# Two transformer branches on one core: first tiles without the keys that do not exist, a bound on rows of short TensorE instructions, and a new set of planner numbers

## The chip, the core and the metric

One core of a Trainium2 chip runs the whole program: one launch, inputs in HBM, output in HBM. The core has five engines with queues of their own: TensorE (PE in the profile; PEld is its weight loading), VectorE (DVE), ScalarE (ACT), GpSimd (POOL) and SyncE (SP), which issues nearly all transfers. The metric is device time in microseconds (us).

## What is computed

`x` is (4, 1024, 256), f32. It is normalised, goes through two independent branches, and the three are added.

```python
x = L0_attn_x
xn = _layernorm(x, axis=-1)
x = x + _L0_attn_ref(xn, ...) + _L0_ffn_ref(xn, ...)

# first branch: rms norm, 16 heads of 64, window 64
scores = einsum('bhnqd,bhnkd->bhnqk', qb, kctx) * scale   # 64 queries, 2 x 64 keys
diff = Bk + qi - kj
base = (diff >= 0) & (diff <= window)
key_exists = (blk - 1) * Bk + kj[None] >= 0
attn = softmax(where(base & key_exists, scores, NEG))
out = einsum('bhnqk,bhnkd->bhnqd', attn, vctx) * sigmoid(gates)
return out.reshape(b, S, HEADS * DIM_HEAD) @ W_out

# second branch: 2 layers, 8 heads of 64, window 128
h = shift_token(x)                       # half the features one token later
q, k, v = split(h @ wqkv)                # q, k: l2 norm, scale, rotation
mask = (i < j) | (i > j + WINDOW) | (j == -1)
attn = softmax(where(mask, -max, q @ k.T));  x = x + (attn @ v) @ wo
h = layernorm(shift_token(x)) * lg + lb
a, g = split(h @ w1 + b1);  x = x + (a * gelu(g)) @ w2 + b2
```

A block of queries sees its own block of keys and the one before. For the first block of a sequence the one before does not exist, and the mask (`key_exists`, `j == -1`) excludes it.

## The kernel before

**Tiling.** The 4 sequences of 1024 tokens are cut into 16 blocks of 256 tokens (`TB`), 4 a sequence (`g` counts them), and each block into 2 tiles of 128 tokens (`i`). `first_attention(n)` does the first branch of block `n`; `layer(l, n)` does the attention of layer `l` of the second branch for block `n`, and `after_attention` its second half. The loops at the end of `layers_kernel` call the first branch for all blocks, then layer 0, then layer 1, with the last three blocks of the first branch mixed with the first of layer 0.

**The planner.** These functions issue nothing. Each calls `op(us, fn, r, w, a, ...)`, which records an operation (`fn` emits its instructions), its estimated time on each engine that can do it, and what it reads and writes. When all are recorded, `Plan.run` simulates the engines with these estimates and fixes one order for each engine and the buffer of each tile; then `Plan.emit` calls the functions in that order. At each step it takes, for each engine, the waiting operation with the smallest `score`: its due time, plus `IDLE` times the time that the engine would stand idle until the operation can begin, plus `TURN` if it needs another mode than the one before (on PE `full` for matmuls on the whole 128x128 array, `rc` for those on 64x64 quarters). `RATE` and `LAND` give a transfer's planned time, `LAT` the delay from an operation's end to its users, `SLACK` a factor on an engine's times, `LOOK` how far ahead in the recorded order an operation may be taken, and the last table of `Plan(...)` how many buffers of a kind are kept for older operations.

**Attention on TensorE.** All matmuls are f32. One matmul of the program shows as two matmul records in the profile, each with a weight load. In the first branch a tile of 128 tokens is done for 4 pairs of heads at a time (`q4`, two groups): `sa` (`scores`, L798) makes the scores, 16 matmuls on 64x64 quarters; DVE adds the mask and takes the minimum (L824); ACT does the exponential (L834); POOL weighs (L853); a transfer out and back and a DVE transpose (`across`, `turn_in`, L464, L473, L481) turn the result; `oa` (`attend`, L887) multiplies by the values, 24 matmuls in three pieces: (1) 128 queries by the keys of the tile, (0) the first 64 queries by the 64 keys before them, (2) the last 64 queries by the last 64 keys. In the second branch a tile has 8 heads: `sb` (L1118), 16 matmuls with 192 key columns (`WB`), the same chain (L1139, L1153, L1173, `across`), and `ob` (L1208), 32 matmuls in four pieces. The first tile of a sequence (`opens`, or `g == 0 and i == 0`) runs the same instructions as any other: keys and values of the missing block are zeros, and a second mask excludes them. L1463 (`last`) is the other place with 64x64 matmuls, 4 for a block.

**Everything else on TensorE** is `full`: projections to queries and keys (L764, `qka`), values and gates (L675, `va`), out (L922, `pr`); in the second branch L979 (`qkvb`), L1233 (`pw`), L1403 (`up`) and L1449 (`down`).

**The start.** `load_x(0)` brings the first block. DVE and POOL make its statistics, DVE normalises it (L643). For blocks 0 and 1 (`EARLY`) `across` is called with `near`: PE transposes the four pieces into a PSUM bank (L427), ACT or DVE copies the bank to the tile `hT` (L452), and `scaled` multiplies `hT` in place by gamma (L658 on ACT). Then the projections begin (L764, L675).

Of the kernel before, what the change touches and what calls it, by code (L numbers as in the profile page):

```python
# [44 lines left out]
N_D = 12  # L45
RATE = 540.0
LAND = 3.7
LAG = 2
# [22 lines left out]
class Op:  # L71
    __slots__ = (
        "us", "fn", "bufs", "mode", "out", "rank", "lat", "left", "ready", "users", "done",
        "start", "end", "eng", "name", "n", "due",
    )


class Plan:
    LAT = {"PE": 0.25, "DVE": 0.30000000000000004, "ACT": 0.30000000000000004, "POOL": 0.30000000000000004, "SP": 2.0}
    SLACK = {"DVE": 1.05, "POOL": 1.05, "ACT": 1.15}  # L80
    SWITCH = {"PE": 0.1, "ACT": 1.4}
    TURN = {"PE": 3.0, "ACT": 40.0}
    IDLE = 300.0
    LOOK = 120.0
    DEAR = {"DVE": 3.0}
# [9 lines left out]

    def op(self, us, fn, r=(), w=(), a=(), mode=None, out=None, lat=None, name=""):


        o = Op()
        o.us, o.fn, o.mode, o.lat, o.name = us, fn, mode, lat, name  # L100
        o.out = out or mode
        o.rank, o.n = self.rank, len(self.ops)
        if "PE" in us:
            self.rank += us["PE"]
        o.users, o.done, o.ready = [], False, 0.0
        deps = set()
        for b in r:
            deps.update(b.writers)
            b.readers.append(o)
        for b in w:  # L110
            deps.update(b.writers, b.readers)
            b.writers, b.readers, b.base = [o], [], [o]
        for b in a:
            deps.update(b.readers, b.base)
            b.writers = b.writers + [o]
        deps.discard(o)
        o.bufs = list({id(b): b for b in (*r, *w, *a)}.values())
        for b in o.bufs:
            b.left += 1
        for d in deps:  # L120
            d.users.append(o)
        o.left = len(deps)
        self.ops.append(o)
        return o

    def run(self):
# [13 lines left out]
        for o in self.ops:  # L140
            if not o.left:
                enter(o)
        oldest, out = 0, []

# [16 lines left out]
        while len(out) < len(self.ops):  # L161
# [4 lines left out]
            for e in engines:  # L166
                picks = []
                for o in waiting[e]:
# [13 lines left out]
                    if turn and e in self.SWITCH:  # L182
                        t += self.SWITCH[e]
                    score = o.due + self.IDLE * (t - at[e]) + (self.TURN[e] if turn else 0.0)
                    picks.append((score, o.n, t, o))
                if picks:
# [9 lines left out]
            for other in o.us:  # L196
                waiting[other].remove(o)
            o.done, o.start, o.end, o.eng = True, t, t + o.us[e] * self.SLACK.get(e, 1.0), e
            at[e] = o.end
# [28 lines left out]
def layers_kernel(  # L228
# [41 lines left out]
        },  # L270
        {"w": (4, 0.1, 30), "g": (1, 0.0, 1), "s": (4, 0.05, 12), "ps": (0, 0.02, 3), "d": (1, 0.0, 1)},
    )
# [31 lines left out]

    load_x(0)

    early = fixed([P, 2], "early")
# [298 lines left out]
    def first_attention(n, before):  # L606
# [44 lines left out]
        hT = buf("w")  # L651
        across(hn, 4, [(hT, lambda b: b.t[:, :512].rearrange("p (k c j) -> p j k c", k=4, j=4), 0, 4)], n in EARLY)

        def scaled(e):
            for c in range(NC):
                at = slice(c * TB, (c + 1) * TB)
                if e == "ACT":
                    nc.scalar.mul(hT.t[:, at], hT.t[:, at], gam.t[:, c : c + 1])  # L658
                else:
                    nc.vector.tensor_scalar_mul(hT.t[:, at], hT.t[:, at], gam.t[:, c : c + 1])  # L660

        op({"ACT": 0.9, "DVE": 0.95}, scaled, r=(gam,), w=(hT,), name="hT")
        H = lambda c, i: hT.t[:, c * TB + i * P : c * TB + (i + 1) * P]
# [87 lines left out]
        for q4 in range(PA // GA):  # L751
# [37 lines left out]
            for i in range(NT):  # L789
# [15 lines left out]

                op({"PE": 0.88}, scores, r=(*qd, *kd, *(() if i else (fk[q4],))), w=pss, mode="rc", name="sa")
                sTs, sm = [], buf("s")
# [69 lines left out]

                def attend(e, po=po, sTs=sTs, vs=vts[i], q4=q4):

                    for n, (k, at, m, to) in enumerate(  # L880
                        ((1, WA, P, 0), (0, 0, WA, 0), (2, 3 * WA, WA, WA))
                    ):
                        for h in range(2):
                            for z in range(2):
                                for j in range(2):
# [4 lines left out]
                                        sTs[j].t[r, h * TB + at : h * TB + at + m],  # L890
                                        start=(h == 0 and n == 0), stop=(h == 1 and n == 2),
                                    )

                op(
                    {"PE": 0.94}, attend,
                    r=(*sTs, *{id(v[q4]): v[q4] for z in vts[i] for v in z}.values()), w=po,
                    mode="rc", name="oa",
                )
# [37 lines left out]
    def layer(l, n, before):  # L936
# [33 lines left out]
        for i in range(NT):  # L970
# [139 lines left out]

            def scores(e, pss=pss, qT=qT, kx=kx):
                for hf in range(2):
                    for u in range(2):
                        for blk in range(2):
                            at = (2 * hf + u) * P + blk * D
                            for j in range(2):
                                r = slice(j * D, (j + 1) * D)
                                nc.tensor.matmul(  # L1118
                                    v2(pss[hf][j], 2, WB)[blk * D : (blk + 1) * D, u],
                                    qT.t[r, at : at + D],  # L1120
                                    v2(kx[hf], 2, 2 * P)[r, u, blk * D : blk * D + WB],
                                    start=True, stop=True,
                                )

            op(
                {"PE": 1.3}, scores, r=(qT, *kx), w=(*pss[0], *pss[1]), mode="rc", name="sb",
            )
            mk = mask_b.t[:, int(opens), :]
            sTs = [[], []]
            for hf in range(2):  # L1130
                sm, exs = buf("s"), []
                for j in range(2):
                    s, ex = buf("w"), buf("w")
                    exs.append(ex)

                    def least(e, s=s, sm=sm, ps=pss[hf][j], hf=hf, j=j, rn=rn, mk=mk):
                        for u in range(2):
                            h = 4 * hf + 2 * u + j
                            nc.vector.tensor_tensor_reduce(  # L1139
                                v2(s, 2, WB)[:, u], v2(ps, 2, WB)[:, u],  # L1140
                                mk, rn.t[:, h : h + 1], BIG,
                                ALU.add, ALU.min, sm.t[:, 2 * j + u : 2 * j + u + 1],
                            )

                    op(
                        {"DVE": 0.69}, least, r=(pss[hf][j], mask_b, rn), w=(s,), a=(sm,),
                        name="min",
                    )


                    def expo(e, s=s, ex=ex, sm=sm, j=j):
                        for u in range(2):
                            nc.scalar.activation(  # L1153
                                v2(ex, 2, WB)[:, u].rearrange("p (a k r) -> p k a r", k=3, a=2),
                                v2(s, 2, WB)[:, u].rearrange("p (k a r) -> p k a r", k=3, a=2),
                                AF.Exp, bias=sm.t[:, 2 * j + u : 2 * j + u + 1], scale=-1.0,
# [11 lines left out]
                for j, ex in enumerate(exs):  # L1168

                    def weigh(e, ex=ex, sm=sm, j=j):  # L1170
                        for u in range(2):
                            at = 8 + 2 * j + u
                            nc.gpsimd.tensor_scalar(  # L1173
                                v2(ex, 2, WB)[:, u], v2(ex, 2, WB)[:, u],
                                sm.t[:, at : at + 1], 1.0, ALU.mult, ALU.mult,
# [6 lines left out]
                    across(  # L1182
                        ex, 3,
                        [(
                            sT,
                            lambda b: bass.AP(
                                tensor=b.t.tensor, offset=b.t.offset,
                                ap=[[*b.t.ap[0]], [16, 4], [P, 3], [WB, 2], [1, 16]],
                            ),
                            0, 3,  # L1190
                        )],
# [4 lines left out]

            def attend(e, po=po, sTs=sTs, v=((vt_old, vs, vt, vs_next), (vs_old, vt_old, vs, vt))):


                for n, (k, at, m, to) in enumerate(  # L1200
                    ((1, P, P, 0), (2, 2 * P, P, 0), (0, 0, D, 0), (3, 3 * P + D, D, D))
                ):
                    for hf in range(2):
                        for u in range(2):
                            for j in range(2):
# [7 lines left out]
                                    sTs[hf][j].t[r, at : at + m],  # L1213
                                    start=(hf == 0 and n == 0), stop=(hf == 1 and n == 3),
                                )

            op(
                {"PE": 1.45}, attend, r=(*sTs[0], *sTs[1], vt, vt_old, vs, vs_old, vs_next), w=po,
                mode="rc", name="ob",
            )  # L1220
# [32 lines left out]
    def after_attention(l, n, w, y2, y2_old, ts):  # L1253
# [213 lines left out]

        op({"PE": 0.45}, down_last, r=(gT[-1], w["w2"][-1]), a=(*pzs.values(),), mode="rc", name="last")
        for i, pz in pzs.items():
# [136 lines left out]
```

## Time and profile before

| | |
|---|---|
| time, median of 3 runs | 1722.07 us (1716.95 to 1726.0) |
| time of the profiled execution | 1720.48 us |
| its span, first to last instruction | 1718.7 us |
| mean granted TensorE clock | 1.000 |
| records of the L798 and L887 groups | 2048 and 3072 |
| records of the L1118 and L1208 groups | 2048 and 4096 |
| PE idle from 0 to 34 us | 9.2 of 34.0 us |
| PE idle from 34 to 530 us | 14.5 of 496.0 us |
| PE idle from 530 to 670 us | 0.8 of 140.0 us |
| PE idle from 670 to 1660 us | 8.2 of 990.0 us |
| PE idle from 1660 us to the end | 6.9 of 58.7 us |

The idle times are the length of a stretch less the busy time that the table of stretches gives for PE. The first stretch is the start, the second the first branch, the third the blocks where both branches are mixed, the fourth and fifth the two layers of the second branch and its end. In the views below, a line of the waits reads: engine, what the waiting instruction writes and its line, who was waited for, then total us, number of waits, longest us. A line of the timeline reads: start, length, engine, line, operation, what is written and read, weights' shape, moving operand's shape, number, and in brackets the idle time before it and who ended it; equal instructions in a row are merged into one line, which shows the shape of the first, and a length runs to the modelled end of the last, so that it overlaps the next start. A line of the chain of waits reads: start, length, what. "issue" is time in which the engine waited for nothing that the profile shows.

### The profile page before, as it was taken

Reading aid. Unit: us, or ns where it says so; the run is one execution under the profiler, and the core shown is the slowest. Engines: PE = TensorE matmul, PEld = TensorE weight load, DVE = VectorE, ACT = ScalarE, POOL = GpSimd, SP = SyncE. Lnnn points to the kernel's source line nnn. Section 1 sums busy time; section 2 is a strip of 40 time slices with the busy share of each in tenths; the row PEclk is TensorE's granted clock in tenths of the full one; section 3 lists DMA queues with packets and bytes.
Section 4 is the critical chain, followed back from the end, with each engine's and each line's share of the span. In section 5 each row is a group of like instructions: output and inputs, shape, how many; then the busy total and the mean of one; then the engine's idle time right before and its main releaser. Section 6 shows DMA issues by size and latency. Waiting matters only on the chain. (4 is left out here: it accounts for less than half of the span.)

```text
span 1718.7 us, 49347 instructions
## 1 busy us (share of the span) xinstructions
PE 1679.1 (98%) x16824; PEld 1278.8 (74%) x16824; DVE 1308.0 (76%) x4487; ACT 1143.4 (67%) x3442; POOL 1207.9 (70%) x2010
## 2 busy tenths in 40 slices
PE   7999999999999999999999999999999999999998
PEld 6787888878877777677677777777766776777787
DVE  5765565555567788899898888898888888888872
ACT  4665666655667776676777666776677667766763
POOL 3744455554459788787688788888787887888840
PEclk9999999999999999999999999999999999999999
DMA  7766578666658887777688888688777777777770
GB/s 225 212 194 167 167 236 224 195 177 185 174 158 229 233 242 212 212 223 208 181 239 233 252 238 243 200 230 231 218 209 216 225 204 224 225 220 212 213 205 29
DMA packets 487387, 357.41 MB, mean 208 GB/s; under 512 B 167639, under 2 KB 424542, under 8 KB 487134
## 3 DMA queue, kind: packets, MB, share of 16 engines
q1 hardware_dynamic: 486430, 354.05, 72.4%
q8 instruction: 132, 2.16, 0.5%
q14 instruction: 121, 0.99, 0.2%
q10 hardware_dynamic: 704, 0.21, 0.0%
HBM read 170.39 MB, written 146.01 MB: 184 GB/s over the span
## 5 line engine op out<-in xcount | busy, mean ns | idle before, releaser
L412 ACT COPY w<-ps 128x512 f32<-128x512 f32 (+2 forms) x661 | 340.7, 582 | 326.1 <-PE ps L764 96.7
L481 DVE STREAM_TRANSPOSE w<-w 128x256 f32<-128x256 f32 (+2 forms) x781 | 455.8, 628 | 104.1 <-DMA w<-d 57.0
L979 PE MATMUL ps<-w,w 128*128 128x512 f32 x768 | 347.2, 595 | 1.4 <-DVE s L1139 0.9
L853 POOL TENSOR_SCALAR w<-w,s,s 128x128 f32<-128x128 f32 x512 | 229.4, 466 | 129.5 <-DVE s L843 107.1
L1403 PE MATMUL ps<-w,w 128*128 128x256 f32 (+1 forms) x1452 | 313.6, 374 | 2.1 <-ACT w L1377 1.1
L1403 PEld LDWEIGHTS ps<-w,w 128*128 128x128 f32 x1452 | 267.7, 190 | 49.5 <-issue 5.2
L1173 POOL TENSOR_SCALAR w<-w,s 128x192 f32<-128x192 f32 x512 | 237.9, 485 | 82.6 <-DVE s L1165 58.8
L403 POOL TENSOR_TENSOR s<-s,mhalf 128x16 f32<-128x16 f32 (+3 forms) x113 | 230.5, 2040 | 77.1 <-DVE s L624 52.2
L1153 ACT ACTIVATE w<-w,s 128x192 f32<-128x192 f32 x512 | 226.4, 444 | 44.8 <-DVE s L1139 11.2
L979 PEld LDWEIGHTS ps<-w,w 128*128 128x128 f32 x768 | 144.1, 190 | 149.5 <-issue 128.6
L1047 POOL TENSOR_TENSOR w<-w,w 128x256 f32<-128x256 f32 x256 | 198.9, 782 | 66.0 <-ACT w L412 48.0
L764 PE MATMUL ps<-w,w 128*128 128x256 f32 x1024 | 229.5, 382 | 1.7 <-DMA w<-in_L_attn_W_qkv_dram 1.7
L764 PEld LDWEIGHTS ps<-w,w 128*128 128x128 f32 x1024 | 195.7, 192 | 34.7 <-issue 2.2
L834 ACT ACTIVATE w<-w,s 128x128 f32<-128x128 f32 x512 | 198.2, 389 | 30.3 <-issue 11.6
L1139 DVE CUSTOM_DVE_ANT_0 w<-ps,mask_b,s 128x192 f32<-128x192 f32 x512 | 181.5, 409 | 9.0 <-PE ps L1118 5.5
L1063 DVE TENSOR_TENSOR w<-w,w 128x256 f32<-128x256 f32 x256 | 139.4, 590 | 48.7 <-ACT w L412 39.5
L1417 ACT ACTIVATE g<-ps,b 128x256 f32<-128x256 f32 (+1 forms) x198 | 87.1, 467 | 93.1 <-PE ps L1403 83.6
L1449 PE MATMUL ps<-w,w 128*128 128x256 f32 x640 | 144.8, 380 | 2.4 <-DVE w L1428 1.1
L1449 PEld LDWEIGHTS ps<-w,w 128*128 128x128 f32 x640 | 120.8, 190 | 30.6 <-issue 7.6
L824 DVE CUSTOM_DVE_ANT_0 w<-ps,mask_a 128x128 f32<-128x128 f32 x512 | 112.4, 284 | 37.0 <-PE ps L798 32.2
L1233 PE MATMUL ps<-w,w 128*128 128x256 f32 x512 | 125.7, 388 | 3.8 <-DVE w L1475 3.0
L1208 PEld LDWEIGHTS ps<-w,w 64*64 64x64 f32 x4096 | 92.0, 133 | 37.3 <-issue 24.5
(85 smaller groups left out, 2473.4 us busy)
## 6 DMA issues: line engine op xcount, KB each, us to landing
d<-w SPq DMA_DIRECT2D x301, 256.0 KB, 3.2
w<-d SPq DMA_DIRECT2D x301, 256.0 KB, 3.8
d<-w SPq DMA_DIRECT2D x256, 192.0 KB, 3.3
w<-d SPq DMA_DIRECT2D x256, 192.0 KB, 3.2
w<-w SPq DMA_DIRECT2D x256, 128.0 KB, 3.3
w<-c SPq DMA_DIRECT2D x81, 256.0 KB, 3.5
c<-w SPq DMA_DIRECT2D x48, 256.0 KB, 3.0
w<-in_L_attn_x_dram SPq DMA_DIRECT2D x16, 256.0 KB, 3.2
```

Of the source, the lines that this page charges most:

```text
L403: nc.gpsimd.tensor_tensor(dst, src, mhalf.t[:, : src.shape[1]], ALU.pow)
L412: nc.scalar.copy(dst(), src())
L481: lambda e, b=b, to=to, at=at, k=k: nc.vector.transpose(to(b), v3(t, 4, m, 32)[:, :, at : at + k]),
L764: nc.tensor.matmul(pq.t[:, j * TB : (j + 1) * TB], W[c].t[:, p % GA * P : (p % GA + 1) * P], hT.t[:, c * TB : (c + 1) * TB], start=(c == 0 ...
L834: nc.scalar.activation(of(ex, u), v2(s, GA, P)[:, u].rearrange("p (k a r) -> p k a r", k=2, a=2), AF.Exp, bias=sm.t[:, at : at + 1], scale ...
L853: nc.gpsimd.tensor_scalar(run(s, u), run(s, u), sm.t[:, at : at + 1], gate.t[:, h : h + 1], ALU.mult, ALU.mult,)
L979: nc.tensor.matmul(p.t, y.t[:, at : at + P], w["wqkv"][m][c].t[:, :512], start=(c == 0), stop=(c == NC - 1),)
L1047: nc.gpsimd.tensor_tensor(rot.t[:, :512].rearrange("p (h u k r) -> p u k h r", h=2, u=2, k=PB)[:, u], raw[m].t[:, :512].rearrange("p (k h ...
L1153: nc.scalar.activation(v2(ex, 2, WB)[:, u].rearrange("p (a k r) -> p k a r", k=3, a=2), v2(s, 2, WB)[:, u].rearrange("p (k a r) -> p k a r ...
L1173: nc.gpsimd.tensor_scalar(v2(ex, 2, WB)[:, u], v2(ex, 2, WB)[:, u], sm.t[:, at : at + 1], 1.0, ALU.mult, ALU.mult,)
L1403: nc.tensor.matmul(pf.t[:, n_ * TB : (n_ + 1) * TB][:, cols], wt, d.t[:, c * TB : (c + 1) * TB][:, cols], start=(c == 0), stop=(c == NC - 1),)
L1449: nc.tensor.matmul(pz.t[:, :DIM], gT[m // 2].t[:, at : at + P], v2(w["w2"][m // 2], 2, DIM)[:, m % 2, :], start=(m == 0), stop=False,)
```

## The change

1. In the first branch, the first tile of a sequence drops piece (0) of `oa`: 8 of its 24 matmuls.
2. In the second branch, the first tile of a sequence leaves out the first 64 of the 192 key columns: in `sb` (128 columns for 192), in the minimum, the exponential, the weighing and the turning (two pieces for three), and `ob` drops two of its four pieces: 16 of its 32 matmuls.
3. Operations with short matmuls get a size `dense`. The planner keeps a sum `row` over such operations, lowered by `REFILL` for each us of other PE work or PE idling; an operation that would bring it over `ROW` has `CROWD` added to its score.
4. At the start DVE sets a tile to zero, and PE multiplies it by itself 7 times into a PSUM bank that nobody reads.
5. For blocks 0 and 1 `scaled` reads the PSUM bank of the transposes; the copy between is gone.
6. Other planner numbers: `RATE`, `LAND`, `LAT`, `SLACK`, `TURN`, `IDLE`, `LOOK`, and how many tiles of kind `w` are kept for older operations.

```diff
-RATE = 540.0
-LAND = 3.7
+RATE = 500.0
+LAND = 3.9
...
-    LAT = {"PE": 0.25, "DVE": 0.30000000000000004, "ACT": 0.30000000000000004, "POOL": 0.30000000000000004, "SP": 2.0}
-    SLACK = {"DVE": 1.05, "POOL": 1.05, "ACT": 1.15}
+    LAT = {"PE": 0.25, "DVE": 0.20000000000000004, "ACT": 0.20000000000000004, "POOL": 0.20000000000000004, "SP": 2.0}
+    SLACK = {"DVE": 1.1, "POOL": 1.05, "ACT": 1.15}
     SWITCH = {"PE": 0.1, "ACT": 1.4}
-    TURN = {"PE": 3.0, "ACT": 40.0}
-    IDLE = 300.0
-    LOOK = 120.0
+    TURN = {"PE": 10.0, "ACT": 60.0}
+    IDLE = 200.0
+    LOOK = 150.0
+    ROW, REFILL = 640, 300.0
+    CROWD = 60.0
...
                     score = o.due + self.IDLE * (t - at[e]) + (self.TURN[e] if turn else 0.0)
+                    if o.dense and row - self.REFILL * (t - at[e]) + o.dense > self.ROW:
+                        score += self.CROWD
...
+            if e == "PE":
+                full = t - at[e] + (0.0 if o.dense else o.us[e])
+                row = max(0.0, row - self.REFILL * full) + o.dense
...
-        {"w": (4, 0.1, 30), "g": (1, 0.0, 1), "s": (4, 0.05, 12), "ps": (0, 0.02, 3), "d": (1, 0.0, 1)},
+        {"w": (3, 0.05, 20), "g": (1, 0.0, 1), "s": (4, 0.05, 12), "ps": (0, 0.02, 3), "d": (1, 0.0, 1)},
...
+    still, idle_bank = fixed([P, TB], "still"), buf("ps")
+    op({"DVE": 0.2}, lambda e: nc.vector.memset(still.t, 0.0), w=(still,))
+
+    def stir(e):
+        for n in range(7):
+            nc.tensor.matmul(
+                idle_bank.t[:, :TB], still.t[:, :P], still.t, start=True, stop=True,
+            )
+
+    op({"PE": 6.0}, stir, r=(still,), w=(idle_bank,), mode="full", name="stir")
...
+        pt = hT
+        if n in EARLY:
+            pt = buf("ps")
+            transposes(
...
-                    nc.scalar.mul(hT.t[:, at], hT.t[:, at], gam.t[:, c : c + 1])
+                    nc.scalar.mul(hT.t[:, at], pt.t[:, at], gam.t[:, c : c + 1])
...
-                op({"PE": 0.88}, scores, r=(*qd, *kd, *(() if i else (fk[q4],))), w=pss, mode="rc", name="sa")
+                op({"PE": 0.88}, scores, r=(*qd, *kd, *(() if i else (fk[q4],))), w=pss, mode="rc", name="sa", dense=128)
...
+                pieces = [(1, WA, P, 0), (0, 0, WA, 0), (2, 3 * WA, WA, WA)]
+                if g == 0 and i == 0:
+                    pieces.pop(1)
...
                 op(
-                    {"PE": 0.94}, attend,
+                    {"PE": 0.94 if len(pieces) == 3 else 0.72}, attend,
...
-                    mode="rc", name="oa",
+                    mode="rc", name="oa", dense=192,
...
+            k0 = 1 if opens else 0
...
-                                    v2(pss[hf][j], 2, WB)[blk * D : (blk + 1) * D, u],
+                                    v2(pss[hf][j], 2, WB)[blk * D : (blk + 1) * D, u, k0:],
...
-                                    v2(kx[hf], 2, 2 * P)[r, u, blk * D : blk * D + WB],
+                                    v2(kx[hf], 2, 2 * P)[r, u, blk * D + k0 : blk * D + WB],
...
-                {"PE": 1.3}, scores, r=(qT, *kx), w=(*pss[0], *pss[1]), mode="rc", name="sb",
+                {"PE": 0.88 if opens else 1.3}, scores, r=(qT, *kx), w=(*pss[0], *pss[1]), mode="rc", name="sb", dense=256,
...
                     across(
-                        ex, 3,
+                        ex, 3 - k0,
...
+            pieces = [(1, P, P, 0), (2, 2 * P, P, 0), (0, 0, D, 0), (3, 3 * P + D, D, D)]
+            if opens:
+                pieces = pieces[1::2]
...
-                {"PE": 1.45}, attend, r=(*sTs[0], *sTs[1], vt, vt_old, vs, vs_old, vs_next), w=po,
-                mode="rc", name="ob",
+                {"PE": 0.72 if opens else 1.45}, attend, r=(*sTs[0], *sTs[1], vt, vt_old, vs, vs_old, vs_next), w=po,
+                mode="rc", name="ob", dense=256,
...
-        op({"PE": 0.45}, down_last, r=(gT[-1], w["w2"][-1]), a=(*pzs.values(),), mode="rc", name="last")
+        op({"PE": 0.45}, down_last, r=(gT[-1], w["w2"][-1]), a=(*pzs.values(),), mode="rc", name="last", dense=32)
```

## The prediction

> **What bounds the kernel now.** First the page: busy shares, and the queues that carry instructions.
>
> ```profile
> PE 1679.1 (98%) x16824; PEld 1278.8 (74%) x16824; DVE 1308.0 (76%) x4487; ACT 1143.4 (67%) x3442; POOL 1207.9 (70%) x2010
> ...
> q8 instruction: 132, 2.16, 0.5%
> ```
>
> TensorE (PE) has work almost all the time, so a microsecond of it saved or lost on PE is one of the span, as long as nothing else comes up. Queue q8 brings code: 2.16 MB for 2 x 16824 PE instructions (each matmul record has one weight load) is 64 bytes an instruction; 132 packets for 33,648 are one packet per 255. So q8 is PE's code, in blocks of some 256 instructions. Second, the waits of PE, the longest:
>
> ```profile
> PE ps L798 <- issue: 9.3, 10, 2.2
> PE ps L427 <- DVE w L643: 7.5, 1, 7.5
> PE ps L887 <- issue: 3.9, 5, 1.5
> ```
>
> 15 waits of 13.2 us in all are for nothing that the profile shows ("issue"), and only at L798 and L887, the short 64x64 matmuls of the first attention. Third, the timeline of PE around one such place, and around one row of the same lines that is shorter:
>
> ```profile
> 206.92 3.97 PE L887 MATMUL ps<-w,w 64*64 64x128 f32 x176
> 211.68 0.46 PE L887 MATMUL ps<-w,w 64*64 64x64 f32 x16 [0.80 <-issue]
> 211.96 3.30 PE L798 MATMUL ps<-w,w 64*64 64x128 f32 x111
> 216.48 0.76 PE L798 MATMUL ps<-w,w 64*64 64x128 f32 x17 [1.21 <-issue]
> 217.17 2.21 PE L922 MATMUL ps<-w,w 128*128 128x256 f32 x9
> ...
> 59.32 2.04 PE L887 MATMUL ps<-w,w 64*64 64x128 f32 x96
> 61.28 2.85 PE L798 MATMUL ps<-w,w 64*64 64x128 f32 x96
> 64.06 5.97 PE L675 MATMUL ps<-w,w 128*128 128x272 f32 x20
> ```
>
> The upper row has 192 + 128 = 320 matmuls, so 640 instructions (2.5 blocks of code), and stops twice. The lower has 192 and doesn't stop: 96 of L887 in 1.96 us (20.4 ns each) and 96 of L798 in 2.78 us (29 ns). I read it thus: short matmuls use code faster than it is brought, and a long row uses up what was brought ahead. Last, the steady part (670 to 1660 us): PE 981.8 busy of 990.0, DVE 856.5, POOL 800.7, DMA share 0.77.
>
> **Part 1: short rows bounded.** The planner gives sa 128 units (32 matmuls), oa 192 (48), sb 256 (32), ob 256 (64), and makes a row over 640 dear. Between 34 and 530 us the old order has 12 rows of four oa and four sa, 1280 units; from first to last start they take 8.7, 9.7, 8.7, 10.3, 7.8, 9.6, 9.4, 11.0, 9.5, 8.6, 8.1 and 8.3 us, 109.6 in all. Without stops one would take 192 x 20.4 ns + 128 x 29 ns = 7.63 us, twelve 91.6. The difference, 18.0 us, is the whole prize (13.2 us in the waits; the rest hides in the modelled ends, some 0.27 us at each stop). Cut in two, a row has 160 matmuls, fewer than the 192 that ran through. Some stops may stay where two halves lie close: I take 16.5 of the 18.0. The price is turns between 64x64 and 128x128 work. The chain of waits has one output projection behind a short row and one behind full work:
>
> ```profile
> 1657.94 1.92 PE ps L1233 x8
> ...
> 1673.22 1.74 PE ps L1233 x8
> ```
>
> 0.18 us to come out of a row; going in adds about 0.1 (20 of L1449 ahead of a short row take 4.41 us in the timeline, 1579.05 to 1583.46; the chain gives them 4.32). 12 more rows x 0.3 = 3.6 us. Net -12.9; bounds -18.0 (every stop gone, the new turns won back elsewhere by TURN 10) and +3.6. In the later part a tile's row is ob + sb (+ last), 512 to 544 units, below the bound already: nothing. [...]
>
> **Part 2: keys that don't exist.** The chain prices rows of the later part:
>
> ```profile
> 1627.84 1.50 PE ps L1208 x64
> 1629.34 1.30 PE ps L1118 x32
> ```
>
> ob (L1208): half of the 64 matmuls go, 32 x 22 ns (the start-to-start of that group, 1.39 us over 64) = 0.70 us; 2 layers x 4 sequences = 8 times: 5.6. sb (L1118): 128 columns for 192; the nearest row is L798, 32 matmuls of 128 columns, 1.03 us with its way out against 1.42 for L1118 with its own: 0.4 x 8 = 3.2. oa (L887): 16 of 48 go, 16 x 20.4 ns = 0.33, for 4 sequences x 2 groups of heads: 2.6. Together -11.4 us, on PE, the bound. Shorter minima, exponentials, weighing and transposing transfers (two of three 128 x 128 pieces) are off the path: ACT, DVE and POOL have a tenth or more free. If a tile's chain is late behind them, this helps too; I count nothing. The planner's own figures (0.22 + 0.42 + 0.73 us, 8 each) give -11.0; the other bound is 0, if the freed time is lost in waits.
>
> **Part 3: the start.**
>
> ```profile
> 7.54 1.35 PE L427 MATMUL ps<-ident,w 128*128 128x128 f32 x4 [7.54 <-DVE w L643]
> 10.57 9.33 PE L764 MATMUL ps<-w,w 128*128 128x256 f32 x32 [1.69 <-DMA w<-in_L_attn_W_qkv_dram]
> 19.74 4.68 PE L675 MATMUL ps<-w,w 128*128 128x272 f32 x16
> 24.26 7.07 PE L764 MATMUL ps<-w,w 128*128 128x256 f32 x32
> ```
>
> The first 32 matmuls of L764 take 9.17 us to the next line, the next 32 6.9; the first four transposes 1.35 us, four at 33.74 0.60. PE begins at a lower rate, which the clock row (1.00 throughout) doesn't show. The zero matmuls (7, so 14 records of 128x256 at about 0.43 us, as when five start in 10.00 to 12.50) run from about 1 to 7 us, while PE waits for DVE until 7.54: they cost nothing if over by then, some 0.5 if not. If they bring the rate up, 2.3 us on L764 and 0.6 on the transposes go. Besides, the copy out of PSUM on ACT (L452, 8.93 to 9.99, 1.06 us) is left out ahead of the scaling at 10.01, which PE waits for; the DMA that the wait names was issued at 1.2 to 3.3 us and lands in 5.5. Sum -3.9, at least -1.1; I take -3.5. [...]
>
> **Part 4: other numbers of the planner** (RATE, LAND, LAT, SLACK, TURN, IDLE, LOOK, spare buffers) change the order everywhere, with no operation added. From below: the waits of PE from 670 to 1660 us are 8.2 us, and 6.9 in the last 58.7, so no more than some 10 can be won. From above: a late tile, rival 2. I take 0: the hops are planned 0.1 us shorter, transfers 0.2 us longer and DVE 5% slower, which about cancels.
>
> **Sum**, against the profiled execution's own 1720.48 us (span 1718.7, 1.8 around it; the median shown is 1722.07, 0.1% above): -12.9 - 11.4 - 3.5 = -27.8, so 1692.7; I say 1693.
>
> **Rivals.** 1. *The rows aren't what stops PE, or aren't cut* (the dearness of 60 is as much as 0.3 us of planned idling at IDLE 200, so with no full work ready the planner lets a row grow). Against it: stops only in rows of 320, none in the 192. For it: a bound of 320 instructions still exceeds a block. The 16.5 stay: 1693 + 16.5 = 1709. 2. *A late tile*: with 0.1 us less allowed on each hop of DVE, ACT and POOL, the chain minimum, exponential, reciprocal, weighing, transfer out and in, turning is planned about 0.8 us too short, and PE waits at the head of its row (L1208) in each of the 64 tiles of the second attention. For it: DVE is 87% and POOL 81% busy there, and single waits of PE reached 1.4 us (L1118 for a copy, L412). Against it: only 8.2 us of waits now. At 0.8 us x 64 = 51 it gives 1744; it undoes the gain from 28 / 64 = 0.43 us a tile. 3. *The new order also closes old waits* (8.2 and 6.9 us above): 1693 - 10 = 1683. 4. *The turns*: sb counts 256 for 32 matmuls, so ob and sb of neighbouring tiles no longer share a row; one more turn in each of 64 tiles, 0.3 x 64 = 19 us: 1712, near the edge of no change. [...]
>
> **Chances.** Forecast 0.50 (own range 1686 to 1701), rival 1 0.16, rival 2 0.09, rival 3 0.17, rival 4 0.08. The range 1679 to 1712 holds the forecast, rivals 1 and 3 and most of 4. A measurement tells some 0.5% (8.6 us) from no change: faster is below 1713.5. Faster: 0.50 + 0.16 + 0.17 + 0.04 = 0.87; same: half of 4 and a mild 2, 0.06; slower 0.07.
>
> **What would show it.** Part 1: no "issue" waits of PE at L798 and L887, no short row over 160 matmuls between 34 and 530 us, some 12 rows more. Part 2: 48 x 8 fewer matmul records (oa 16, ob 32) and 14 more for the zeros; L1118 in two forms. Part 3: the first 32 of L764 in some 7 us, begun near 9. Wrong if "issue" stays, if L764 starts at the slow rate again, or if PE's waits for DVE, ACT or DMA from 670 us on exceed 8.2 us by much.

## The result, and the profile after

The changed kernel takes 1696.31 us (median of 4 runs, 1694.46 to 1697.68), against 1720.11 us for the kernel before beside it: a ratio of 0.9861, 95% interval 0.984 to 0.9881. The span of its profiled execution is 1694.2 us, 24.5 less than before; the forecast was 27.8 less.

The page of the changed kernel, busy time and the queue that brings PE's code (L798 is now L825, L887 L917, L764 L791, L1118 L1150, L1208 L1242, L1233 L1267, L979 L1009):

```profile
PE 1669.5 (99%) x16454; PEld 1269.0 (75%) x16454; DVE 1288.3 (76%) x4508; ACT 1121.9 (66%) x3417; POOL 1192.5 (70%) x2013
...
q8 instruction: 129, 2.11, 0.5%
```

There are 370 fewer matmul records: 384 for the keys left out, 14 more for the zeros. The waits of PE, from the longest:

```profile
PE ps L1483 <- DVE w L1462: 3.3, 3, 1.2
PE ps L1267 <- ACT w L431: 3.1, 6, 1.1
PE ps L791 <- ACT w L431: 1.7, 5, 0.4
PE ps L1267 <- DVE w L1509: 1.4, 1, 1.4
PE ps L446 <- DVE w L662: 1.3, 1, 1.3
PE ps L320 <- DVE still L316: 1.2, 1, 1.2
PE ps L1267 <- issue: 1.1, 1, 1.1
```

The 13.2 us of "issue" at L798 and L887 are gone. One such wait of 1.1 us is left, at an output projection (L1267); no packet of q8 ends in the 2.5 us ahead of its end, so it does not look like the old stops, and its cause is open. From the start of each short matmul of these two lines to the next start on PE, all together, the old order spends 142.6 us and the new one 127.0. The timeline of PE at two neighbouring rows shows one row of 192 and one of 128 without a stop, with full work between them:

```profile
272.20 4.10 PE L917 MATMUL ps<-w,w 64*64 64x128 f32 x192
276.41 7.17 PE L952 MATMUL ps<-w,w 128*128 128x256 f32 x32
283.52 3.72 PE L825 MATMUL ps<-w,w 64*64 64x128 f32 x128
```

And the start:

```profile
1.17 5.35 PE L320 MATMUL ps<-still 128*128 128x256 f32 x14 [1.17 <-DVE still L316]
7.87 1.00 PE L446 MATMUL ps<-ident,w 128*128 128x128 f32 x4 [1.34 <-DVE w L662]
9.79 7.17 PE L791 MATMUL ps<-w,w 128*128 128x256 f32 x32 [0.93 <-ACT w L685]
16.80 4.60 PE L702 MATMUL ps<-w,w 128*128 128x272 f32 x16
21.24 7.07 PE L791 MATMUL ps<-w,w 128*128 128x256 f32 x32
```

The second group of 32 projections begins at 21.24 us, 24.26 before: 3.0 us won at the start. The number of rows of short matmuls on PE went from 92 to 109, from 15 to 30 of them between 34 and 530 us. Two lines of the table of stretches (the stretch, its length, then busy time and number for PE, PEld, DVE, ACT and POOL, the granted clock, the share of the transfers and GB/s) give PE's idle time in the first branch, 4.0 us instead of 14.5, and in the second, 10.4 instead of 8.2:

```profile
34.00:530.00 496.00, 492.00 (x5808) 403.22 (x5804) 310.00 (x1530) 313.10 (x1205) 275.05 (x606) 1.00 0.70 198
670.00:1660.00 990.00, 979.62 (x8669) 715.05 (x8668) 839.03 (x2470) 686.64 (x1832) 787.82 (x1181) 1.00 0.76 217
```

### The profile page after: what moved, and what is told of

Its sections match the earlier page's. It is cut to its first block, busy times and chain, and to the rows that moved or that the text cites. A ratio compares the mean times of both kernels' runs of the same rounds, so it can differ in the third digit from the quotient of the medians.

```text
span 1694.2 us, 48683 instructions
## 1 busy us (share of the span) xinstructions
PE 1669.5 (99%) x16454; PEld 1269.0 (75%) x16454; DVE 1288.3 (76%) x4508; ACT 1121.9 (66%) x3417; POOL 1192.5 (70%) x2013
## 4 chain that ended last, share of the span: by engine, by line
PE 53%; POOL 3%; DVE 1%; ACT 1%; issue 1%; DMA 1%; SPq 0%; POOLq 0%; DVEq 0%; ACTq 0%
PE ps L1437 17%; PE ps L1009 14%; PE ps L1483 7%; PE ps L1267 6%; PE ps L1242 4%; PE ps L1150 4%; POOL w L1077 1%; PE ps L1497 1%; POOL s L422 1%; POOL w L1205 1%; ACT w L431 1%; DMA w<-d 0%; DMA out_dram<-w 0%; POOL w L1101 0%; DMA sc<-in_L_ffn_k_scale_dram 0%
## 5 line engine op out<-in xcount | busy, mean ns | idle before, releaser
L431 ACT COPY w<-ps 128x512 f32<-128x512 f32 (+3 forms) x624 | 327.7, 585 | 329.7 <-PE ps L791 96.3
L500 DVE STREAM_TRANSPOSE w<-w 128x256 f32<-128x256 f32 (+2 forms) x781 | 450.5, 621 | 95.7 <-DMA w<-d 35.8
L1009 PE MATMUL ps<-w,w 128*128 128x512 f32 x768 | 347.6, 595 | 1.7 <-DVE w L1467 0.7
L1437 PE MATMUL ps<-w,w 128*128 128x256 f32 (+1 forms) x1452 | 312.0, 373 | 1.1 <-ACT w L431 1.1
L1437 PEld LDWEIGHTS ps<-w,w 128*128 128x128 f32 x1452 | 268.3, 190 | 45.5 <-issue 5.9
L1205 POOL TENSOR_SCALAR w<-w,s 128x192 f32<-128x192 f32 (+1 forms) x512 | 230.7, 471 | 91.8 <-DVE s L1197 85.7
L1185 ACT ACTIVATE w<-w,s 128x192 f32<-128x192 f32 (+1 forms) x512 | 223.0, 439 | 48.1 <-DVE w L500 11.2
L1009 PEld LDWEIGHTS ps<-w,w 128*128 128x128 f32 x768 | 144.3, 190 | 147.3 <-issue 127.0
L791 PE MATMUL ps<-w,w 128*128 128x256 f32 x1024 | 230.3, 381 | 2.9 <-ACT w L431 1.7
L791 PEld LDWEIGHTS ps<-w,w 128*128 128x128 f32 x1024 | 193.0, 190 | 37.1 <-ACT w L431 3.9
L1171 DVE CUSTOM_DVE_ANT_0 w<-ps,mask_b,s 128x192 f32<-128x192 f32 (+1 forms) x512 | 177.9, 402 | 15.4 <-PE ps L1150 4.9
L1093 DVE TENSOR_TENSOR w<-w,w 128x256 f32<-128x256 f32 x256 | 125.8, 537 | 27.4 <-ACT w L431 21.1
L1483 PEld LDWEIGHTS ps<-w,w 128*128 128x128 f32 x640 | 120.9, 190 | 30.7 <-issue 9.9
L1267 PE MATMUL ps<-w,w 128*128 128x256 f32 x512 | 126.6, 390 | 6.7 <-ACT w L431 3.1
L1267 PEld LDWEIGHTS ps<-w,w 128*128 128x128 f32 x512 | 92.7, 189 | 35.7 <-ACT w L431 15.7
```

The source lines that it names most:

```text
L431: nc.scalar.copy(dst(), src())
L500: lambda e, b=b, to=to, at=at, k=k: nc.vector.transpose(to(b), v3(t, 4, m, 32)[:, :, at : at + k]),
L791: nc.tensor.matmul(pq.t[:, j * TB : (j + 1) * TB], W[c].t[:, p % GA * P : (p % GA + 1) * P], hT.t[:, c * TB : (c + 1) * TB], start=(c == 0 ...
L1009: nc.tensor.matmul(p.t, y.t[:, at : at + P], w["wqkv"][m][c].t[:, :512], start=(c == 0), stop=(c == NC - 1),)
L1185: nc.scalar.activation(v2(ex, 2, (3 - k0) * D)[:, u].rearrange("p (a k r) -> p k a r", k=3 - k0, a=2), v2(s, 2, WB)[:, u, k0 * D :].rearra ...
L1205: nc.gpsimd.tensor_scalar(v2(ex, 2, m)[:, u], v2(ex, 2, m)[:, u], sm.t[:, at : at + 1], 1.0, ALU.mult, ALU.mult,)
```

## The experiments

In every experiment the time of the kernel before was taken beside it. Three kernels keep the order of every engine exactly as it was, so that they show one thing alone (`no_zeros`, `all_keys`, `old_order_fewer_keys`); the others make the planner find a new order. `...` in a diff stands for lines left out. Differences to the changed kernel are between runs of different sessions, partly on another chip; where that matters, the ratios to the kernel before beside each are compared instead.

**The zero matmuls, order kept.**

```diff
-        for n in range(7):
+        for n in range(0):
```

> The changed kernel with the same order on every engine, but the 7 zero matmuls are not issued. Theory (they bring PE's rate up before the first projection): the first 32 records of L791 take 9.2 us again instead of 7.0 and the four transposes 1.35 instead of 1.0, and all that follows is later by 2.3 to 2.9 us: a span near 1696.5 to 1697 (1694.2 with them). Rival (the early start comes from the copy left out alone, and the rate from something else in the order): the first block of L791 stays at 7.0 us and the span at 1694 +- 1.

Measured: 1698.53 us, ratio 0.9877 (0.9861 to 0.9893); span 1694.7 us. The times are 2.2 us apart by the medians, but the intervals of the two ratios overlap. The timeline separates the kernels, at the start and in the mixed part:

```profile
7.81 1.35 PE L446 MATMUL ps<-ident,w 128*128 128x128 f32 x4 [7.81 <-DVE w L662]
10.08 8.64 PE L791 MATMUL ps<-w,w 128*128 128x256 f32 x32 [0.93 <-ACT w L685]
18.56 4.60 PE L702 MATMUL ps<-w,w 128*128 128x272 f32 x16
...
648.63 1.99 PE L1437 MATMUL ps<-w,w 128*128 128x256 f32 x8 [1.58 <-ACT w L431]
```

The zeros bring the rate up, as the theory has it: without them the first block is slow again (8.64 us instead of 7.17), and L702 starts 1.76 us later. The trace's first record of a full clock begins at 13.09 us without the zeros and at 5.38 us with them. The same matmul that starts at 645.36 us with zeros starts at 648.63 without, 3.3 us later (two short rows also stopped at other places, for 1.0 us). Between 1009 and 1105 us 2.3 us of that lag are given back, mostly in waits of L1267 for ACT and DVE that are shorter or absent in the late kernel, and at the end of these two executions 0.5 us is left, where the rival had it. But the profiled execution without zeros was the fastest of its four: the median of the four spans is 1696.5 us against 1694.3 with zeros, 2.2 apart, which is the theory's figure. So an early gain can be given back where other engines are late too; how much of it is lost as a rule is not shown.

**The bound on rows, taken out.**

```diff
-    CROWD = 60.0
+    CROWD = 0.0
```

> The changed kernel with CROWD at 0, so that the planner orders without the bound on rows. Theory (rows of more than some 200 short matmuls run out of code): rows of 320 come back in the first attention, PE's waits for nothing shown come back at L825 and L917 with 10 us or more, and the time rises by 12 to 17 us, to 1708 to 1713. Rival 1 (the other numbers of the planner, TURN 10 and IDLE 200, shape the rows): rows stay short and the time stays within 3 us of 1696. Rival 2 (long rows come back, but what stopped them was not code): no such waits in spite of rows of 320, and the time falls by 3 us, as turns are saved.

Measured: 1708.83 us, ratio 0.9932 (0.9918 to 0.9947), so 12 us more than the changed kernel. The waits of PE, and the timeline of one row:

```profile
PE ps L825 <- issue: 6.3, 9, 1.2
PE ps L917 <- issue: 2.9, 4, 1.4
```

```profile
317.11 3.85 PE L917 MATMUL ps<-w,w 64*64 64x128 f32 x174
321.78 0.50 PE L917 MATMUL ps<-w,w 64*64 64x64 f32 x18 [0.82 <-issue]
322.07 3.30 PE L825 MATMUL ps<-w,w 64*64 64x128 f32 x109
326.58 0.87 PE L825 MATMUL ps<-w,w 64*64 64x128 f32 x19 [1.21 <-issue]
```

Rows of 288 and 320 and their stops are back, and the two lines take 139.1 us instead of 127.0, which by itself is the 12 us. The theory holds; 9.2 us of waits are a little under its 10.

**All keys, order kept.** The changed kernel as planned, but the first tiles use every key:

```diff
-            k0 = 1 if opens else 0
+            k0, told = 0, 2 if opens else None
...
-            if opens:
-                pieces = pieces[1::2]
...
```

> The changed kernel planned with the same costs, so the same order on every engine, but the first tiles of a sequence use all their keys again (sb, minimum, exponential, weighing, transfers, ob and oa as for any other tile). Theory (all of this work on PE lies on the path): +11.4 us, so 1707 to 1708, and 384 more matmul records than the changed kernel. Rival (the planned order leaves room where the work was, or the added short matmuls and transfers make late tiles): less than +6, or more than +16 us.

Measured: 1709.65 us, ratio 0.9941 (0.9925 to 0.9956): 13 us more by the medians, 10.7 by the spans of the profiled executions (1704.9, the fastest of four), and 16838 records, 384 more. The theory holds, with a part that it did not have: moved by the added instructions, three rows stop for code again ("issue" at the first branch's values, 3.2 us).

**Rows by themselves.** Only rows of short matmuls between full work, without and with transfers.

```diff
...
+    def row_160():
+        for k in range(160):
+            one(k)
...
```

> Nothing of the reference is computed (the output is zeros): only rows of 64x64 matmuls with 64 columns on PE, none of which waits for another engine, between 80 matmuls (160 records, some 34 us) of the whole array: rows of 96, 192 and 320 records, twice 160 records with 8 or with 32 records of full work between, and one of 1280; first without transfers, then once more while SP writes 256 KB pieces to HBM all the time. Theory (code is brought in blocks of 256 instructions, slower than short matmuls use it, with little ahead): the rows of 96 and 192 run through at 20 to 22 ns a record; the row of 320 stops once or more for 1 to 2 us; two rows of 160 with 8 records between stop, with 32 between they hardly do; the row of 1280 settles at about 4.2 us for 128 records, 33 ns each. [...] Rival B (code is late only while other transfers run): no stops in the first half, stops in the second.

Measured, in one execution: span 654.1 us. The timeline of PE, first the row of 1280 records without transfers, then the row of 320 with transfers of 285 GB/s (from 440 to 456 us):

```profile
244.73 2.44 PE L113 MATMUL small<-z 64*64 64x64 f32 x151
248.49 2.09 PE L113 MATMUL small<-z 64*64 64x64 f32 x128 [1.32 <-issue]
251.94 2.09 PE L113 MATMUL small<-z 64*64 64x64 f32 x128 [1.36 <-issue]
255.40 2.09 PE L113 MATMUL small<-z 64*64 64x64 f32 x128 [1.36 <-issue]
...
442.40 2.67 PE L113 MATMUL small<-z 64*64 64x64 f32 x167
447.15 2.09 PE L113 MATMUL small<-z 64*64 64x64 f32 x128 [2.08 <-issue]
451.98 0.84 PE L113 MATMUL small<-z 64*64 64x64 f32 x25 [2.73 <-issue]
```

Once it has stopped, PE stops again after every 128 records, which are 256 instructions, one block of q8. From one stop to the next it takes 3.5 to 4.0 us without transfers and 4.8 with them (447.15 to 451.98), though a block's own matmuls need some 2.1. The packets of q8 in the traces show that these are waits for code: all 26 stops of this run end 1.2 to 1.6 us after a packet of 16,384 bytes (256 instructions of 64 bytes) has ended, and so do the 15 stops of the kernel before, 1.2 to 1.5 us after one. In the first long row the next packet begins 1.05 to 1.14 us after PE goes on; under the transfers it begins 2.0 to 2.6 us after, and the stops there are longer by about as much (2.73 us for a full block against 1.32 to 1.91). I read it thus: a block of short matmuls is used in 2.1 us and comes every 3.5 to 4.0, so a row goes on only as long as the code that is there ahead of PE lasts. The first stops of the rows of 320 and 1280 came after 151 to 223 records, 302 to 446 instructions, less than two blocks. Rival B falls as the only cause: under transfers the stops are longer, but they come without them too. The second long row began at 584.5 us, after the transfers had ended, so no long row was seen under them. One thing in the theory was wrong: the length of a row alone does not decide. A row of 192 stopped once for 1.17 us before its last record without transfers and ran through with them. Without transfers the two rows of 160 with 8 records between ran through, and of the two with 32 between one stopped for 1.61 us, the other way round than expected. That it depends on where the blocks' edges fall in a row is my reading; no run sets the edges alone.

**The bound alone, in the kernel before.** The row bookkeeping and the `dense` sizes added, nothing else.

```diff
+    ROW, REFILL = 640, 300.0
+    CROWD = 60.0
...
```

> The kernel before with one thing of the change, the bound on rows (dense, ROW 640, REFILL 300, CROWD 60); all keys, old start, old numbers. Theory (the bound stands by itself): rows of 320 are gone, PE's waits for nothing shown at L798 and L887 fall from 13.2 us to below 3, and the time falls by 10 to 15 us, to 1705 to 1710. Rival 1 (it needs the new numbers, TURN 10 above all, or loses elsewhere what it wins): the time falls by less than 5 us. Rival 2 (the gain of the changed kernel's order is from the numbers): no fall.

Measured: 1715.7 us, ratio 0.9965 (0.9954 to 0.9977). The rows of 320 are gone, the stops are down to two of 0.8 us together, and the two lines take 131.5 us instead of 142.6, 11 less. But the time falls by 6 only: between the theory and rival 1. There are 111 rows instead of 92, PE's idle time went from 0.8 to 2.9 us between 530 and 670 us and from 8.2 to 10.1 between 670 and 1660, and L1241 (the old L1233) waits for DVE 5.3 us instead of 3.0.

**Old planner numbers with all the rest changed**, and **new numbers alone** in the kernel before.

```diff
-RATE = 500.0
-LAND = 3.9
+RATE = 540.0
+LAND = 3.7
...
-    TURN = {"PE": 10.0, "ACT": 60.0}
-    IDLE = 200.0
-    LOOK = 150.0
+    TURN = {"PE": 3.0, "ACT": 40.0}
+    IDLE = 300.0
+    LOOK = 120.0
...
```

The diff is that of the first kernel; the second has the reverse of it in the kernel before.

> The changed kernel with the old RATE, LAND, LAT, SLACK, TURN, IDLE, LOOK and spare buffers; bound, keys and start as changed. Theory (the new numbers are worth nothing by themselves): 1696 +- 4 us. Rival 1 (the numbers carry a good part of the gain): 1702 or more. Rival 2 (the numbers cost what the sum is short of, 27.8 forecast against 24.5 us of span): 1692 or less.

> The kernel before with the new planner numbers alone; no bound, all keys, old start. Theory (they only reorder, and with 10 for a turn rows of 320 and their stops stay): 1720 +- 5 us, PE's waits for nothing shown 9 to 16 us. Rival 1 (better fitting numbers close PE's other waits): 1712 or less. Rival 2 (less time allowed on the hops makes late tiles in the second branch): 1730 or more, with PE's waits for DVE, ACT and POOL after 670 us doubled.

Measured: the old numbers give 1717.95 us, ratio 0.9981 (0.9969 to 0.9993); the new numbers alone 1726.53, ratio 1.0031 (1.0014 to 1.0049). Both fall outside the theory, the second by 1.5 us only, and its stops came as expected (11.2 us): alone the new numbers cost some 5 us, and without them the other three parts win almost nothing. The waits of PE under the old numbers, from the longest:

```profile
PE ps L1267 <- DVE w L1509: 7.5, 9, 1.2
PE ps L917 <- DVE w L500: 3.0, 2, 1.8
PE ps L791 <- DVE w L687: 2.4, 1, 2.4
```

Output projections (L1267) wait nine times for an addition on DVE (L1509), in the second branch; the changed kernel waits there once. The two lines below it are mostly one place: between 575 and 581 us PE stands still for 1.85 and 2.37 us, and the trace has the clock at half for 6.8 us from 578.5 us on. PE's idle time from 530 to 670 us is 8.1 us instead of 1.5.

**Which numbers**: one weight, and the four time estimates.

```diff
-    TURN = {"PE": 10.0, "ACT": 60.0}
+    TURN = {"PE": 3.0, "ACT": 60.0}
```

The diff is that of the weight; the other kernel has the old RATE, LAND, LAT and SLACK.

> The changed kernel with one number old: 3 for a turn of PE instead of 10. The planner then orders 141 rows of short matmuls instead of 109. Theory (once rows are bounded, TURN decides how far they are cut up; this number carries much of what the old numbers lose): 32 more rows at 0.3 us are 10 us, and with them PE's waits for DVE and ACT grow: 1706 to 1718. Rival (the old numbers lose by their time estimates, not by this): within 4 us of 1696.

> The changed kernel with the old time estimates (RATE 540, LAND 3.7, LAT 0.3, DVE SLACK 1.05) and the new weights (TURN, IDLE, LOOK, spare buffers). Theory (estimates that let DVE look quicker make tiles late: PE's output projection, L1267, waits for DVE again): 1702 to 1714, and waits of L1267 for DVE above 4 us in place of 2.2. Rival (the estimates are worth nothing, the weights all): within 4 us of 1696.

Measured: 1734.78 us for the turn, ratio 1.0074 (1.0047 to 1.01); 1716.53 us for the estimates, ratio 0.9963 (0.9948 to 0.9978). Both theories have the sign, both too little. With 3 for a turn PE has 141 rows instead of 109, 20 of the 32 more between 670 and 1660 us, and one wait that explains a good part of the rest:

```profile
36.22 0.66 PE L446 MATMUL ps<-ident,w 128*128 128x128 f32 x4
46.42 9.44 PE L791 MATMUL ps<-w,w 128*128 128x256 f32 x32 [9.54 <-DVE w L687]
```

PE stands still for 9.5 us ahead of the second block, and the block after it takes 9.4 us instead of 7.1, at a lower rate. With the old estimates no such place stands out: L1267 waits for DVE 2.2 us, not above 4, so that half of the theory fell; PE's idle time from 670 to 1660 us is 17.8 us (10.4 in the changed kernel), spread over L1267, L1150, L1242, L1437 and L1009. Why these orders make many tiles a little late was not settled further.

**A new order that means nothing.**

```diff
-RATE = 500.0
+RATE = 503.0
```

> The changed kernel with RATE 503 in place of 500, which says nothing new of the chip but moves three of four operations to another place in the planner's order. It measures what a new order alone is worth. Theory (orders from these numbers differ by little): 1696 +- 4 us. Rival (any new order is good or bad for 10 us and more, so that differences of that size between the kernels prove nothing): outside 1688 to 1706.

Measured: 1704.25 us, ratio 0.9895 (0.9869 to 0.9922), 8 us more than the changed kernel by the medians and 6 by the ratios, as the kernel before was 2.5 us slower beside this run. That is outside the theory and short of the rival, which needed more than 1706. It is one such order, so it gives no bound; but differences of less than some 8 us between kernels in different orders say little. The bound's 12 us, the estimates' 20 (17 by the ratios) and the turn's 38 (37) stand above it; the 6 us of the bound alone and the 5 of the numbers alone do not. Part of the 8 is seen at the start, in the table of stretches of the nudged kernel and of the changed one:

```profile
9.85:13.26 3.41, 3.41 (x9) 2.76 (x10) 0.00 (x0) 0.03 (x1) 0.00 (x0) 0.54 0.84 266
```

```profile
9.85:13.26 3.41, 3.41 (x16) 3.02 (x17) 0.00 (x0) 0.59 (x1) 0.53 (x2) 1.00 0.88 257
```

The columns are the stretch, its length, busy time and number for PE, PEld, DVE, ACT and POOL, the granted clock, the share of the transfers and GB/s. In the same 3.41 us PE begins 9 matmuls at a clock of 0.54 or 16 at 1.00, with the same instructions on PE before. That costs 1.7 us (8.86 against 7.17 for the first block of L791). Three other orders with the same start kept the rate (7.17 us for that block in `no_bound`, `all_keys` and `old_numbers`), so this part need not come from the order.

**A tighter bound.**

```diff
-    ROW, REFILL = 640, 300.0
+    ROW, REFILL = 512, 300.0
```

> The changed kernel with ROW at 512: 128 records, so one block of code. Theory (a row that doesn't reach over more than one whole block can't stop, wherever it lies; longer ones stop or not by where the blocks' edges fall): no stop at L825 and L917, but some 6 to 12 more rows in the first branch at 0.3 us each, as rows of 160 lose little now: 1696 to 1700. Rival (the rows of 144 to 192 still lose some 5 us or more in the changed kernel): 1693 or less.

Measured: 1728.47 us, ratio 1.0049 (1.0031 to 1.0066). The times of both theory and rival are far off. No stop at L825 and L917 is left, as the theory had it, in rows of up to 224 records; but the two lines take 127.1 us against 127.0 in the changed kernel, so there was nothing to win. There are 149 rows, 40 more than in the changed kernel, where 6 to 12 were expected, so some 12 us of turns at 0.3 each; near the end one projection waits 5.1 us for ACT (L1437 for L1411), and the clock is at 0.53 in the 3.6 us from 1672.0; and the first block of L791 takes 1.7 us longer. That is some 20 of the 32 us; the rest was not followed up. One row of ob and sb is 512, so with `last` (32) it no longer fits, and the second branch's rows are cut as well (90 instead of 63 between 670 and 1660 us).

**Fewer keys in the old order, order kept.** The kernel before, planned with all keys, leaves them out.

```diff
+            k0 = 1 if opens else 0
...
+            if opens:
+                pieces = pieces[1::2]
...
```

> The kernel before with its own order on every engine, but the first tiles of a sequence leave out the keys that don't exist (planned as if they didn't). Theory (PE is the bound in the old order too): -11.4 us, 1709 to 1711, with 384 fewer matmul records. Rival (the old order has other engines near the bound in the second branch, and waits take up what PE saves): less than 7 us, 1714 or more.

Measured: 1716.45 us, ratio 0.9961 (0.9943 to 0.9979): 6 us less, so the rival; the interval (3.6 to 9.8 us) leaves out the theory's 11.4. It has 384 fewer records, but PE's idle time from 670 to 1660 us rose from 8.2 to 12.7 us; the longest waits there:

```profile
PE ps L1240 <- DVE w L1482: 5.2, 6, 1.4
PE ps L1240 <- ACT w L412: 2.6, 3, 1.0
```

These were 3.0 and 0.5 us before. I read it thus: PE came to its output projections earlier and found DVE and ACT no earlier. The idle time accounts for 4.5 us; the stops for code stayed (13.0 us of waits). The same keys, taken out of an order planned for that, are worth 11 to 13 us.

## Why the prediction was right, and where it was not

The time forecast was 1693 us, and it is 1696.3. Step by step:

- **Part 1, rows, -12.9.** Right in the mechanism, and near in size. Taking the bound out costs 12 us. The two lines became 15.6 us shorter, 2.6 of it the keys' by the forecast's own price; the 13.0 that are left hold the ways out of the new rows, for which the forecast was 16.5 less 12 x 0.18, or 14.3. There are 17 more rows instead of 12. The reading (code is brought in blocks and late in long rows) was shown by the rows alone and by the packets of q8: 26 stops there, each 1.2 to 1.6 us after a packet had ended.

  Some things were taken too simply. Short rows are not safe by their length: in the rows alone one of 192 records stopped for 1.17 us and one of 160 for 1.61, and others of the same lengths ran through. "No row over 160" did not come true (four rows of 192), as the bound makes an operation dearer and doesn't forbid it. "Only at L798 and L887" left out a wait for "issue" of 0.2 us at L1233 in the same view. And the row times given as "first to last start" run to the next start behind the row (to the last start they are 107.2 us in all).
- **Part 2, keys, -11.4.** Right in the new order (10.7 by the spans, 13 by the medians, with 3.2 us of stops that came back in it). In the old order some half of it is lost, to waits for DVE and ACT; the bound that was given for this, 0, was the right kind.
- **Part 3, the start, -3.5.** 3.0 us in the profiled execution. Leaving out the copy won 0.8 us, not 1.06 (PE's wait behind the transposes went from 1.69 to 0.93); it has no run of its own. L791 began at 9.79 us, not near 9, because DVE's normalisation, which the transposes wait for, began 0.3 us later (7.40 against 7.07), and the scaling on ACT still takes 0.9 us behind them.

  Of the eight profiled executions here whose kernels issue the zeros, four had the first block of L791 in 7.17 us (the changed kernel, `no_bound`, `all_keys`, `old_numbers`) and four in 8.59 to 8.86 (`old_estimates`, `row_512`, `turn_3`, `nudged`). The length of PE's pause does not explain it: from the end of the zeros to L791 it was 2.6 to 3.1 us in the four that fell and 3.3 to 3.8 in the four that kept the rate. What goes with the outcome is the clock: its first full stretch began at 4.1 to 5.4 us in the four that kept it and at 6.0 to 6.7 in those that fell, and in its first 3.41 us PE had 1.1 to 1.8 us of zero matmuls and projections against 0.7 to 0.9. These are eight kernels with one profiled execution each; that the same kernel goes both ways is likely but not shown. So a start at the lower rate is as likely as the forecast of this part, and costs some 1.7 us; it does not come with zeros that end early, as they ended later (6.8 to 7.2 us) where the rate fell than where it stayed (5.9 to 6.5).
- **Part 4, the planner's numbers, 0.** This step failed. It was argued that they cancel, with no more than 10 us to be won. In fact they decided in these runs whether the rest pays: with the old numbers the other parts give 0.2%, with the old TURN alone the kernel is slower than before, with the old estimates it wins 0.4%. Why the old numbers' orders make tiles late is open, and so is a rival that no run tests: that the new numbers stand for one good order, of which a nudge already loses 6 to 8 us. Taken out one at a time, the parts add up once the new numbers are in: 1726.5 (numbers alone) less 13 (keys), 12 (rows), 2 (zeros) and 1 (the copy, from the trace) is about 1698. That the sum of the forecast, which put the numbers at 0, came out within 4 us is in part luck, as one meaningless change of the order moved the time by more.
- **Rival 4 (turns)** was given a small chance and is no part of the result (63 rows from 670 to 1660 us, 62 before), but its mechanism is what `turn_3` and `row_512` show, with 83 and 90 rows there. **Rival 2 (late tiles)** was expected of the new numbers; it is the old ones that show it in part.
- The 3.3 us by which the span falls short: PE's idle time from 670 to 1660 us is 10.4 us instead of 8.2, and the start gave 0.5 less; the rest lies within what a new order is worth.

## What to carry to other kernels

PE was 98% busy here and still had 13.2 us of stops for code: look at such an engine's waits for "issue" and at the length of rows of short instructions, and count instructions against the packets of its code queue. Where a planner or any other search fixes the order, its numbers are not a neutral part of a change: test each part with the order kept, and test once what an order that means nothing is worth, here 6 to 8 us, before a smaller difference is read as a cause. Work taken off the bound engine paid in full here only where the other engines had been planned to be there earlier as well.

## What the runs showed of the hardware that was not expected

- PE stopped after every 128 short matmul records (256 instructions), from stop to stop 3.5 to 4.0 us without transfers and 4.8 us under 285 GB/s; each stop ended 1.2 to 1.6 us after a packet of 16,384 bytes on q8. With the order kept and the code shifted against the rows the stops moved: leaving out 28 instructions brought two back (`no_zeros`, 1.0 us), adding 768 brought three (`all_keys`, 3.2 us).
- The rate of PE, once up, fell again in four of the eight executions with the zeros. In them the full clock had begun at 6.0 to 6.7 us, and in its first 3.41 us PE had 0.7 to 0.9 us of zero matmuls and projections; in the four that kept the rate it had begun at 4.1 to 5.4 us, with 1.1 to 1.8 us of them. What of this decides was not shown. The clock of the table of stretches shows the fall: 0.54 from 9.85 to 13.26 us in `nudged`, 0.50 from 9.85 to 13.20 us in `row_512` and 1.00 there from 13.30 us on. The slow start of the kernel before shows only in the durations there, since the trace's first clock record begins at 14.98 us and the table gives 1.00 where there is none.
